# FFN's way down in a decoder layer: half chunk's weights padded to 128 rows, a quarter of the casts on GpSimd

## Chip, cores and metric

One core of a Trainium2 chip runs the whole kernel in one launch. The metric is the device time in microseconds. Engines are called as the profile calls them: PE (TensorE matmul), PEld (TensorE weight load), DVE (VectorE), ACT (ScalarE), POOL (GpSimd), SP (SyncE, which only issues DMAs here).

## What is computed

A decoder layer over x of shape 4 x 1024 x 256: windowed causal self-attention, cross-attention to 77 context rows, and a quantised feed-forward network (FFN) with 704 hidden units. The change touches the FFN's last matrix product alone. The reference, cut to the FFN:

```python
def _act_fake_quant(x, clip_factor):
    scale = sigmoid(clip_factor) * max(abs(x)) / 127
    return clip(round(x / scale), -128, 127) * scale

xq = _act_fake_quant(layernorm(x), clip_x[0])          # 4 x 1024 x 256
gate = xq @ weight_quant(w_gate).T                     # 704 hidden units
up = xq @ weight_quant(w_up).T
h = _act_fake_quant(silu(gate) * up, clip_down[0])     # one scale over all of h
x = x + h @ weight_quant(w_down).T                     # back to 256
```

The scale of h comes from the largest absolute value of all of h, so the way down can begin only when the last h is there.

## The kernel before

Tokens are cut into 32 tiles of 128; eight groups n of four tiles (512 tokens) go through the FFN. The 704 hidden units are five full chunks of 128 (`FULL` = 5) and a half chunk of 64 (`HR` = 64). The half chunks of two groups, an even n and the odd one after it, share one slot of 128 rows: rows 0 to 63 belong to the even group, rows 64 to 127 to the odd one. So a pair m of groups has 11 slots in `hT` (float32): slots 0 to 4 and the shared slot 5 are treated with the even group, slots 6 to 10 with the odd one.

The weights of the way down are `wdT`, bf16, 128 rows x 6 chunks x 256. In its sixth chunk the 64 rows of the half chunk stand twice, in rows 0 to 63 and again in rows 64 to 127, so that each group's matmul finds weights on the rows of its own data. They are made by DVE during attention.

Stages of the FFN, as they follow in time: `act_scale` for the input; `gate_up` for n = 0 to 7, in which POOL widens the inputs from int8 to bf16 (L1199); `act_scale` for h; and the way down. The order on each engine is the order of the program text, each engine has its own queue, and engines wait for each other by semaphores.

The way down runs over ten parts: `(0, 2)`, `(2, 2)`, six parts of four tiles (groups 1 to 6), and two parts of two tiles again. For each part `quantised_h` has ACT write int8 (`h8`, L1323) and DVE cast it to bf16 (`hq`, L1324), one instruction of each for a whole part (the first part has one for each of its two tiles). `down` then does six matmuls for each token tile (L1338), with 128 columns of `hq` as weights and 256 columns of `wdT` streamed; two tiles share a PSUM bank `po`. DVE multiplies the bank by the row of scales (L1343). Of the four tiles of a part the first two are then stored by a DMA that adds to the output in memory, issued by POOL (L1347); for the other two DVE adds x (L1349) and SP issues a plain store (L1350). The last two parts both use the second way. `quantised_h` is called one part ahead of `down`, so DVE's queue holds: cast of part k+1, product, product and sum of part k, cast of part k+2. `h8` and `hq` have two buffers each, one for a pair of groups, and `y` has six.

In `down` the sixth matmul of each tile works on 64 rows: the even group's on rows 0 to 63, the odd group's on rows 64 to 127.

Of the kernel before, what the change touches and what calls it, by code (L numbers as in the profile page):

```python
# [9 lines left out]
BF16 = mybir.dt.bfloat16  # L10
# [7 lines left out]
P = 128  # L18
# [6 lines left out]
def decoder_layer(  # L25
# [32 lines left out]
    nc = tc.nc  # L58
    B, S, D = x.shape
# [9 lines left out]
    HT = NT // NH  # L69
# [3 lines left out]
    HR = FF - (NF - 1) * P  # L73
# [66 lines left out]
    wdT = fw.tile([P, NF, D], BF16, name="wdT")  # L140
# [44 lines left out]
    with ExitStack() as att:  # L185
# [14 lines left out]
        for o in range(NS):  # L200
# [15 lines left out]
            q = wp.tile([P, 1], F32, name=f"qrows{o}")  # L216
# [8 lines left out]
        f = stage.tile([P, P], F32, name="cb_f", tag="stage")  # L225
# [198 lines left out]
        def prep_ffn():  # L424
# [61 lines left out]
            for w, dst, sc in ((w_gate, wgT, gsc), (w_up, wuT, usc)):  # L486
                for f in range(NF):
                    pieces.append(rows_of(w, dst, sc, f))
            return pieces + [down(c) for c in range(NC)]


# [646 lines left out]
    with ExitStack() as ffn:  # L1138
        ffn.enter_context(tc.manual_schedule(engines=None))
        fp = ffn.enter_context(tc.tile_pool(name="fp", bufs=1))  # L1140
# [34 lines left out]
        FULL = NF - 1  # L1175
# [44 lines left out]
        def largest(k, h):  # L1220
            nc.vector.tensor_reduce(
                hmax[:, k : k + 1], h, AX.XY, ALU.max, apply_absolute_value=True
            )

        def gate_up(n, steps):
# [34 lines left out]
            elif n < NB - 1:  # L1260
                largest(n, hT[:, m, FULL:, :])

        def rows_out(t0):
            b, t = divmod(t0, NT)
            return out[b, t * P : (t + 2) * P, :].rearrange("(t p) d -> p t d", p=P)


        for t0 in range(0, B * NT - 4, 4):
            nc.sync.dma_start(out=rows_out(t0), in_=xb[t0 // NT][:, t0 % NT : t0 % NT + 2, :])
# [38 lines left out]
        def quantised_h(t0, nt, step):  # L1308

            n, i0 = divmod(t0, HT)  # L1310
            m, odd = divmod(n, 2)
            if m not in pairs:
                shape = [P, 2 * FULL + 1, HS]
                pairs[m] = (
                    fwk.tile(shape, I8, name="h8"),
                    fwk.tile(shape, BF16, name="hq"),
                )
            q8, q = pairs[m]

            fs = slice(FULL + 1, None) if odd else slice(0, FULL + 1)  # L1320
            for i in range(i0, i0 + nt, step):
                s = slice(i * P, (i + step) * P)
                nc.scalar.activation(q8[:, fs, s], hT[:, m, fs, s], AF.Copy, scale=ih)  # L1323
                nc.vector.tensor_copy(q[:, fs, s], q8[:, fs, s])  # L1324
            return q

        def down(q, t0, nt):
            odd = t0 // HT % 2
            half = slice(odd * HR, (odd + 1) * HR)
            for t2 in range(nt // 2):  # L1330
                po = ps_f.tile([P, 2, D], F32, name="po", tag="b")
                for i in range(2):
                    at = (t0 + 2 * t2 + i) % HT
                    s = slice(at * P, (at + 1) * P)
                    for f in range(NF):
                        r = half if f == FULL else slice(0, P)
                        k = FULL if f == FULL else odd * (FULL + 1) + f
                        nc.tensor.matmul(  # L1338
                            po[:, i, :], q[r, k, s], wdT[r, f, :], start=(f == 0), stop=(f == FULL)
                        )  # L1340
                b, t = divmod(t0 + 2 * t2, NT)
                y = fwk.tile([P, 2, D], F32, name="y", bufs=6)
                nc.vector.tensor_tensor(  # L1343
                    y, po, dsc_row.unsqueeze(1).to_broadcast([P, 2, D]), ALU.mult
                )
                if t % 4 == 0 and t0 < B * NT - 4:
                    nc.gpsimd.dma_start(out=rows_out(t0 + 2 * t2), in_=y, accum_op=ALU.add)  # L1347
                else:
                    nc.vector.tensor_tensor(y, y, xb[b][:, t : t + 2, :], ALU.add)  # L1349
                    nc.sync.dma_start(out=rows_out(t0 + 2 * t2), in_=y)  # L1350
# [5 lines left out]
        for i, (t0, nt) in enumerate(parts):  # L1356
            ahead.append((quantised_h(t0, nt, nt if i else 1), t0, nt))
            if i == 0:
                nc.vector.tensor_scalar(dsc_row, dsc_row, sh, nokey, ALU.mult, ALU.add)
            if len(ahead) == 2:  # L1360
                down(*ahead.pop(0))
        down(*ahead.pop(0))


# [47 lines left out]
```

## Time and profile before

| | |
|---|---|
| median of three runs | 717.52 us (715.24 to 720.91) |
| the profiled execution | 717.03 us, its span 715.3 us |
| mean granted PE clock | 0.971 |
| way down, first ACT instruction to last DVE instruction | 678.28 to 711.85 us of the span |
| ACT L1323, 11 instructions | 20.93 us without a break, from 678.28 |
| DVE L1324 casts | 560 ns (768 elements) to 1849 ns (3072 elements), 11 instructions |
| PE L1338 | 192 matmuls, 160 on 128 rows and 32 on 64 rows |
| POOL L1347 | 7 DMA issues, about 1.2 us each |
| POOL L1199, int8 to bf16 | 7 casts of 1024 elements, about 1.04 us each |

The span runs from the first to the last instruction of the profile; the time of the execution holds 1.7 us more. Times in what follows are microseconds from the start of the span. A row of a timeline has the start, the duration, the engine, the line, the operation, output and inputs, shapes and count, and in brackets how long the engine sat idle before it and what it waited for. "issue" means that it waited for nothing that the profile shows. Rows that follow without a hole are merged, and a merged row carries the shape of its first member.

### The profile page before, as it was taken

The numbers are of one execution on the slowest core, as the hardware profiler recorded it, in microseconds if no ns is written. First come the engines' busy times: TensorE is split into PE (matmuls) and PEld (weight loads), VectorE is DVE, ScalarE is ACT, GpSimd is POOL, SyncE is SP. The second block draws the span as 40 slices with busy tenths as digits, with TensorE's granted clock in tenths as the row PEclk, the third lists the DMA queues.
The fourth block names the chain that finished last, engine by engine and source line by source line (L and its number), as shares of the span: only waits on it lengthen the run. The fifth ranks groups of instructions, "written<-read, shape, count | busy, mean of one in ns | idle before, by whom it ended". The sixth has DMA issues, their size and how long they took to land.

```text
span 715.3 us, 17054 instructions
## 1 busy us (share of the span) xinstructions
PE 651.2 (91%) x6337; PEld 393.0 (55%) x6342; DVE 565.7 (79%) x1997; ACT 366.3 (51%) x671; POOL 241.7 (34%) x390
## 2 busy tenths in 40 slices
PE   7989999999999889999998998999999996678396
PEld 4557566667665656654566666544544525334153
DVE  5588879669787898667879978877866788689897
ACT  2534555634656436544564454346345382698391
POOL 4035533535335457600155577113400021111022
PEclk9999999999999999999999999999999999699788
DMA  8000100000000000000000000000000000000057
GB/s 290 5 2 11 35 3 17 2 19 18 24 11 1 10 10 11 18 3 16 3 10 23 25 24 23 3 3 4 17 17 4 17 17 15 1 0 1 0 89 148
DMA packets 18644, 17.00 MB, mean 24 GB/s; under 512 B 3788, under 2 KB 18049, under 8 KB 18561
## 3 DMA queue, kind: packets, MB, share of 16 engines
q1 hardware_dynamic: 16369, 14.08, 6.3%
q0 software_dynamic: 1904, 1.84, 2.1%
q8 instruction: 50, 0.82, 0.5%
q14 instruction: 33, 0.27, 0.1%
q10 hardware_dynamic: 288, 0.00, 0.0%
HBM read 9.35 MB, written 6.03 MB: 22 GB/s over the span
## 4 chain that ended last, share of the span: by engine, by line
PE 71%; DVE 17%; ACT 6%; issue 4%; DMA 1%; POOL 0%; ACTq 0%; DVEq 0%
PE ps_p L570 12%; PE sc_n L614 8%; PE ps_av L743 7%; PE sc_t L699 7%; PE ps_op L793 7%; PE sc_n L629 4%; PE ps_av L753 4%; PE sc_t L728 4%; PE ps_v L551 3%; PE po L1338 3%; PE sc_t L684 3%; DVE junk L644 3%; PE ps_t L529 2%; PE pg L1236 2%; PE sc_n L595 1%
## 5 line engine op out<-in xcount | busy, mean ns | idle before, releaser
L644 DVE CUSTOM_DVE_ANT_0 junk<-sc_n,cboth 128x256 bf16<-128x256 f32 (+1 forms) x512 | 172.8, 403 | 36.8 <-PE sc_n L614 36.5
L709 ACT ACTIVATE pt<-sc_t 128x512 f32<-128x512 f32 (+1 forms) x256 | 125.4, 576 | 100.0 <-PE sc_t L699 99.1
L713 POOL TENSOR_SCALAR_AFFINE_SELECT pt<-pt 128x256 f32<-128x256 f32 x256 | 102.8, 410 | 135.8 <-ACT pt L709 125.1
L731 ACT ACTIVATE ptx<-sc_t 77x512 f32<-77x512 f32 x128 | 65.5, 592 | 78.7 <-PE sc_t L728 78.7
L152 POOL TENSOR_TENSOR r<-ve,neghalf 128x4 f32<-128x4 f32 x22 | 22.6, 1028 | 211.9 <-DVE ve L150 136.7
L699 PE MATMUL sc_t<-q,k 32*128 32x256 f32 (+1 forms) x1024 | 87.2, 380 | 1.4 <-DVE mx L644 0.6
L614 PE MATMUL sc_n<-k,q 32*128 32x256 f32 (+1 forms) x1024 | 81.4, 394 | 1.1 <-DVE mx L644 1.1
L655 DVE TENSOR_REDUCE mx<-sc_n 128x4 f32<-128x308 f32 x128 | 52.2, 470 | 31.2 <-PE sc_n L629 31.2
L699 PEld LDWEIGHTS sc_t<-q,k 32*128 32x128 f32 x1024 | 66.8, 189 | 11.8 <-ACT q L584 2.3
L514 POOL TENSOR_SCALAR xn<-x,mv,rs 128x256 f32<-128x256 f32 x56 | 69.6, 1250 | 7.9 <-DVE rs L163 7.9
L614 PEld LDWEIGHTS sc_n<-k,q 32*128 32x128 f32 x1024 | 49.9, 187 | 31.6 <-DVE mx L644 13.0
L570 PE MATMUL ps_p<-xnT,w_s 128*128 128x512 f32 x128 | 62.5, 618 | 2.3 <-DVE mx L644 1.1
L743 PE MATMUL ps_av<-pt,vt 128*32 128x256 f32 (+1 forms) x1152 | 58.6, 346 | 6.2 <-DVE mx L644 4.4
L762 DVE STREAM_TRANSPOSE o_sb<-ps_av 128x512 f32<-128x512 f32 x64 | 45.7, 715 | 20.2 <-PE ps_av L743 11.8
L743 PEld LDWEIGHTS ps_av<-pt,vt 128*32 128x32 f32 x1152 | 34.8, 109 | 33.7 <-DVE mx L644 6.2
L644 DVE DVE_READ_ACCUMULATOR2_ANT mx<- 128x1 f32 x512 | 42.6, 83 | 0.1
L629 PEld LDWEIGHTS sc_n<-kx,q 32*128 32x128 f32 x1024 | 31.5, 186 | 14.5 <-issue 14.5
L684 PE MATMUL sc_t<-mb_t,ident_bf 77*77 77x512 bf16 x128 | 35.4, 379 | 4.1 <-ACT q L580 3.6
L570 PEld LDWEIGHTS ps_p<-xnT,w_s 128*128 128x128 f32 x128 | 22.5, 192 | 28.3 <-issue 17.3
L1250 DVE SCALAR_TENSOR_TENSOR hT<-pu,usc,act 128x512 f32<-128x512 f32 x44 | 30.6, 744 | 8.7 <-ACT act L1249 5.8
L629 PE MATMUL sc_n<-kx,q 32*128 32x77 f32 x1024 | 36.2, 277 | 0.0
L753 PE MATMUL ps_av<-ptx,vx 77*32 77x512 f32 x256 | 35.2, 604 | 0.5 <-DVE mx L655 0.5
(184 smaller groups left out, 1046.4 us busy)
## 6 DMA issues: line engine op xcount, KB each, us to landing
x<-in_x_dram SPq DMA_DIRECT2D x8, 512.0 KB
out_dram<-y SPq DMA_DIRECT2D x9, 256.0 KB
q<-mxT SPq DMA_DIRECT2D x128, 4.0 KB
out_dram<-x SPq DMA_DIRECT2D x7, 256.0 KB
out_dram<-y POOLq DMA_DIRECT2D x7, 256.0 KB, 4.5
w_s<-in_L_attn_w_qkv_dram SPq DMA_DIRECT2D x2, 384.0 KB
raw_d<-in_L_ffn_w_down_dram SPq DMA_DIRECT2D x2, 352.0 KB
raw_f<-in_L_ffn_w_gate_dram SPq DMA_DIRECT2D x5, 128.0 KB
```

Source lines behind the costliest of these rows:

```text
L514: eng.tensor_scalar(xn, xb[job.b][:, t, :], job.st[hf].mv[:, i, 0:1], job.st[hf].rs[:, i : i + 1], ALU.subtract, ALU.mult,)
L570: nc.tensor.matmul(ps, w[:, c, g * P : (g + 1) * P], job.xnT[hf][:, c, :], start=(c == 0), stop=(c == NC - 1),)
L614: nc.tensor.matmul(banks[j][:, (i + 1) * 2 * P - n : (i + 1) * 2 * P], q[r, t * P : (t + 1) * P], k[r, k0 * P : k0 * P + n], start=True, s ...
L629: nc.tensor.matmul(banks[j][:, i * SK : (i + 1) * SK], q[r, t * P : (t + 1) * P], k[r, :], start=False, stop=(i == HT - 1),)
L644: nc.vector.tensor_tensor_reduce(out=junk[:, 2 * P - n :], in0=banks[j][:, (i + 1) * 2 * P - n : (i + 1) * 2 * P], in1=cboth[:, 2 * P - n ...
L684: nc.tensor.matmul(banks[j][:SK], ident_bf[:SK, :SK], mb_t[:, s], start=True, stop=False)
L699: nc.tensor.matmul(banks[j][:, w : w + n], k[r, t * P : (t + 1) * P], q[r, t * P : t * P + n], start=True, stop=True,)
L709: nc.scalar.activation(pt.rearrange("p i a q -> p (i a q)")[:, :w], banks[j][:, :w], AF.Exp)
L713: nc.gpsimd.affine_select(out=pt[:, :, 0, :], in_=pt[:, :, 0, :], compare_op=ALU.is_ge, fill=0.0, base=0, pattern=[[0, 2], [1, P]], channe ...
L731: nc.scalar.activation(pt, banks[j][:SK], AF.Exp)
L743: nc.tensor.matmul(ps[j * SL : (j + 1) * SL, (a0 - t0) * P : (a1 - t0) * P], slot_of(job.vs[kb // 2][:, kb % 2], heads[j]), job.pts[g, o, ...
L753: nc.tensor.matmul(ps[j * SL : (j + 1) * SL, :], slot_of(vx[:, job.b], heads[j]), job.pts[g, o, j, hf], start=True, stop=True,)
```

## The change

A new tile `wdP` of 128 rows x 2 x 256 in bf16 is set to zero by POOL, and POOL copies into it the half chunk's weights: into its first half the rows 0 to 63, into its second half the rows 64 to 127. In `down` the sixth matmul of a tile then reads all 128 rows of the shared slot of `hq`, and the zeros drop the rows of the other group. In `quantised_h`, in the six parts of four tiles, DVE casts only the first three tiles; POOL casts the fourth. The parts of two tiles are cast by DVE alone, as before.

```diff
+        wdP = fp.tile([P, 2, D], BF16, name="wdP")
+        nc.gpsimd.memset(wdP, 0.0)
+        for k in range(2):
+            r = slice(k * HR, (k + 1) * HR)
+            nc.gpsimd.tensor_copy(wdP[r, k, :], wdT[r, FULL, :])
+
         def rows_out(t0):
...
                 nc.scalar.activation(q8[:, fs, s], hT[:, m, fs, s], AF.Copy, scale=ih)
-                nc.vector.tensor_copy(q[:, fs, s], q8[:, fs, s])
+
+                mine = slice(i * P, (i + 3) * P) if step == HT else s
+                nc.vector.tensor_copy(q[:, fs, mine], q8[:, fs, mine])
+                if step == HT:
+                    nc.gpsimd.tensor_copy(q[:, fs, 3 * P :], q8[:, fs, 3 * P :])
             return q
 
         def down(q, t0, nt):
             odd = t0 // HT % 2
-            half = slice(odd * HR, (odd + 1) * HR)
...
                     for f in range(NF):
-                        r = half if f == FULL else slice(0, P)
                         k = FULL if f == FULL else odd * (FULL + 1) + f
                         nc.tensor.matmul(
-                            po[:, i, :], q[r, k, s], wdT[r, f, :], start=(f == 0), stop=(f == FULL)
+                            po[:, i, :],
+                            q[:, k, s],
+                            wdP[:, odd, :] if f == FULL else wdT[:, f, :],
+                            start=(f == 0),
+                            stop=(f == FULL),
                         )
```

POOL's new instructions stand in its queue as follows: the three that fill `wdP` behind its last work of attention (the power at L921) and ahead of its casts of the inputs (L1199); the cast of part k+1 behind the store issue of part k-1 and ahead of that of part k. The numbers of lines in the text are those of the kernel before.

## The prediction

> **What bounds the kernel now.** The page shows PE at 91% and DVE at 79% of the span, but the edited code runs only in the last 37 us. I read the busy time by windows there first; its columns are the busy time and number of instructions of each engine, then the granted PE clock, the DMA share and GB/s.
>
> ```profile
> core 0: us, PE busy (x) PEld busy (x) DVE busy (x) ACT busy (x) POOL busy (x), PEclk, DMA share, GB/s
> 606.00:678.28 72.28, 47.89 (x253) 22.61 (x258) 60.43 (x76) 49.55 (x83) 7.29 (x7) 0.85 0.00 1
> 678.28:686.60 8.32, 6.33 (x33) 3.36 (x34) 5.80 (x8) 8.32 (x6) 1.41 (x1) 0.67 0.04 5
> 686.60:704.45 17.85, 17.85 (x126) 10.22 (x124) 17.64 (x21) 12.61 (x6) 5.76 (x5) 1.00 0.82 147
> 704.45:711.85 7.40, 5.30 (x37) 2.97 (x36) 6.56 (x10) 0.00 (x0) 1.47 (x2) 0.94 0.86 178
> 711.85:715.30 3.45, 0.00 (x0) 0.00 (x0) 0.01 (x1) 0.00 (x0) 0.00 (x0) 0.50 0.22 76
> ```
>
> From 686.60 to 704.45 both PE (17.85 of 17.85) and DVE (17.64) are full: two engines share the bound. Before that ACT is full: it writes the int8 h and lets everything else wait. The chain of waits says the same, and at its end it goes back to DVE:
>
> ```profile
> 681.50 2.33 ACT h L1323
> ...
> 683.86 1.50 DVE hq L1324
> ...
> 685.41 20.83 PE po L1338 x144
> ...
> 707.59 0.96 DVE hq L1324
> ...
> 708.60 1.81 PE po L1338 x12
> ```
>
> Of PE's 20.83 us, what is work? The timeline of the weight loads:
>
> ```profile
> 684.80 0.09 PEld L1338 LDWEIGHTS <-hq 64*128 64x128 bf16 x1 [0.21 <-issue]
> 685.40 0.44 PEld L1338 LDWEIGHTS <-hq 128*128 128x128 bf16 x5 [0.51 <-DVE hq L1324]
> 686.05 0.66 PEld L1338 LDWEIGHTS <-hq 64*128 64x128 bf16 x6 [0.21 <-issue]
> 686.92 0.65 PEld L1338 LDWEIGHTS <-hq 64*128 64x128 bf16 x6 [0.21 <-issue]
> ```
>
> Six loads fill 0.65 us without a hole, then 0.21 us pass in which PE waits for nothing shown; a token tile takes 0.866 us. A group is named by its first member: the hole stands ahead of the 64-row load (alone at 684.80), and none stands ahead of the five 128-row loads behind it. 24 tiles make 5 us of holes.
>
> DVE's own timeline gives its pitch (start to start) from one cast to the next:
>
> ```profile
> 697.36 1.58 DVE L1324 CAST hq<-h 128x2560 bf16<-128x2560 int8 x1
> 698.86 1.27 DVE L1343 TENSOR_TENSOR y<-po,dsc_row 128x512 f32<-128x512 f32 x2
> 700.16 0.69 DVE L1349 TENSOR_TENSOR y<-y,x 128x512 f32<-128x512 f32 x1
> 700.77 1.85 DVE L1324 CAST hq<-h 128x3072 bf16<-128x3072 int8 x1
> ```
>
> Casts of whole parts start at 686.60, 690.30, 693.76, 697.36 and 700.77, and the first of the last two half parts at 704.45: pitches 3.70, 3.46, 3.60, 3.41, 3.68. Inside one: cast 1.42 to 1.77, the two products 1.31, the sum 0.61.
>
> **The change, part by part.**
>
> *64-row matmul becomes 128-row.* All six matmuls of a tile then have one shape, and the hole ahead of the odd one goes: 0.21 us per tile, so a part of four tiles takes 4 x 0.65 = 2.6 us on PE instead of 3.46. On PE alone that is 24 x 0.21 = 5.0 us. It can't be had: DVE needs over 3 us per part and becomes the only bound. So this edit pays only where DVE waited for PE: the two products of the first two whole parts took 1.42 and 1.43 instead of 1.31 (0.23 in all); in the tail the products at 705.42 and 706.26 led to the sum at 706.98, 1.56 instead of 1.31 (0.25); and the last two tiles' matmuls, on the chain at 708.60, lose two holes (0.41). Sum 0.89.
>
> *DVE casts three of four tiles.* The cast lasts 1523 ns for 2560 elements and 1787 for 3072, so 0.516 ns per element. A quarter of a part is 640 or 768 elements: 0.33 or 0.40 us. Six whole parts are cast so; the first of the six (at 683.86) and the start of the second (at 686.60) are held by ACT's h, which is no earlier, so what is won before 686.60 is worth nothing: ACT's chain from 678.28 covers it (0.35 us if that cover were gone). The other five, from 686.60 on, save 0.40+0.33+0.40+0.33+0.40 = 1.86.
>
> *POOL casts the fourth tile.* L1199 is the same operation, int8 to bf16, on POOL: 1042 ns for 1024 elements, so 0.65 or 0.78 us. Other POOL rows are dearer: the affine select at L713 takes 410 ns for 256 elements (1.23 us for 768), the scaling at L514 1250 ns for 256 (3.1 or 3.75 us). I take L1199, which is nearest in kind and types, and keep the others for the range. POOL's new work per part is 0.7 us beside the 1.2 us of the store's issue (L1347), in a pitch of 3.2: there is room. PE needs the fourth tile 3 x 0.65 = 1.96 us after it starts the part, and it starts when DVE's cast ends, so POOL may be over a microsecond late. PE's wait on POOL has only the next part's matmuls behind it. POOL's cast waits for ACT, and behind it in POOL's queue stands the issue of the preceding part's store; for that nobody waits but the end, as y has six buffers. ACT rewrites a pair's h two pairs on: at 689 it needs POOL's cast of about 686.5, at 694 that of about 692, so it does not wait.
>
> *The two casts at once.* The trace has no POOL cast beside a DVE cast. It does have POOL's store issue running into DVE's casts: at 690.30 and 693.76 by 0.13 to 0.18 us, at 697.36 and 700.77 by 0.27, and those two lasted 1.58 and 1.85 against 1.49 and 1.75. So 0.27 us of overlap cost 0.09. In the new order y's first product, 0.3 us of latency and 1.2 of issue again reach 0.25 us into the next cast; I charge 0.09 to the two casts that did not have it yet (0.18). POOL's cast stands behind that issue, so DVE's cast starts first, POOL's falls at worst behind it, beside DVE's products, and is over 0.7 us after DVE's cast: before the fourth tile is due. I price it at 0. If POOL came first and DVE had to wait for all of it, DVE would lose about 0.6 us per part: 3.0 us over five parts, the other end.
>
> The Trainium skill ("SBUF — State Buffer", section "Who interferes with whom") speaks against the change: a DVE cast that uses two ports and any GpSimd instruction share a port pair, and the later one stands still until the earlier has ended. By that rule whoever starts first decides, and the sum would be the forecast or the second rival below; the 0.09 us above is all that a row here shows of it.
>
> *wdP.* POOL sets 512 elements (rows of L249 and of the identity: 592 ns for 578, 205 for 128, so 0.54) and copies twice 256 (0.26 each by L1199, 1.25 by L514): 1.1 to 3.0 us. POOL has nothing to do from 604.00, after its power at L921, to 615.23, its first cast; these 11 us hide it. Without them xq would be late by that much. DVE's small instructions from 604 to 609 are on the path and may be disturbed: 0 to 1.25, I take 0, since POOL is most likely through while DVE reduces maxima at 605.1 to 606.5. No gain can come from it: nothing is removed there.
>
> *Sum.* 1.86 + 0.23 - 0.18 up to the cast at 704.45 (now 702.54), then 0.25 + 0.41: 2.57 us. The last sum on DVE ends near 709.3 instead of 711.85; behind it the last store needs the same 3.45. SP's other stores leave earlier, DMA's share rises from 0.82 to about 0.9 and still does not bind. The profiled execution took 717.03 us (span 715.3, 1.7 around it): **714.5**. It lies 0.5 below the median of the three runs, 717.52, which would give 715.0.
>
> **Rivals.**
>
> *POOL wins the race.* If POOL's cast starts ahead of DVE's, part after part, 3.0 us are given back: 717.03 - 2.57 + 3.0 = 717.5, no change. For it: the issue ends only 0.25 us after DVE's cast starts, a thin margin. Against: the order of the queues, and that margin repeated in five rows.
>
> *POOL is slow and becomes the bound: slower.* Place: POOL's queue, cast and store issue in turn. By L514 a cast takes 3.1 or 3.75; with 1.2 of issue and 0.1 between, a part takes 4.7 instead of 3.57. From 685.3 the six casts and five issues end at 711.2; then the last whole part's fourth tile (0.8), product and sum (1.3), the last cast (1.0), matmuls (1.5), product and sum (1.4): 717.2 for 711.85, so 717.03 + 5.4 = 722.4. It decides from a cast of about 1.9 us, where POOL's part exceeds 3.2. Against it: L1199's seven casts, all within 1037 and 1044 ns.
>
> *The hole stays.* If it does not come from the shape, PE keeps 0.866 per tile: only 0.2 to 0.3 is won at the start, where the first whole part begins earlier: 716.8. Against: the hole stands ahead of the 64-row load alone, and the same engine's 128-row stream at L1236 shows none.
>
> **How the numbers follow.** Forecast 0.62 (its own range 713.0 to 716.5), POOL first 0.16, slow POOL 0.11, hole stays 0.06, else 0.05. Low end: 2.57 + 0.18 + 0.35 all won is 713.9, less the 1.8 by which the lowest run lay under the profiled one: 712.0. High end: 717.5 for the second case plus 2 of run scatter, which also takes in half of the slow-POOL case: 719.5. One per cent, about what a measurement of this kernel can tell from no change, is 7.2 us; no case reaches it, and only scatter or something unseen would: faster 0.06, same 0.88, slower 0.06.
>
> **What would show it.** Right: PE loads of one shape with no 0.21 hole but with waits on DVE's hq in every part; DVE casts of 1.2 and 1.4 us, pitch near 3.2, no idle time; the cast of the first half part near 702.5; POOL casts of 0.65 to 0.8. Wrong: DVE casts or sums stretched by 0.5 or more, POOL casts over 1.9, PE waiting for POOL, or a later start of the stage at 678.28.

## The result, and the profile after

The changed kernel takes 719.16 us (median of 22 runs) against 717.38 us of the kernel before (22 runs): ratio 1.003, 95% interval 1.0019 to 1.0042. It is slower by about 2 us, where 2.6 us less were forecast. The time lies within the stated range, at its upper end, but the sign is the opposite one. The profiled execution took 719.40 us, span 717.7. The new line numbers: L1330 ACT's int8 write, L1333 DVE's cast, L1335 POOL's cast, L1347 the matmuls, L1356 the products, L1360 POOL's store issue, L1362 the sums.

The busy time by windows of the changed kernel, the columns as before:

```profile
678.00:686.60 8.60, 5.83 (x36) 4.07 (x37) 5.93 (x10) 8.23 (x6) 2.17 (x2) 0.67 0.08 5
686.60:704.45 17.85, 12.66 (x111) 10.22 (x108) 17.71 (x18) 12.70 (x7) 8.66 (x9) 1.00 0.64 118
704.45:714.00 9.55, 5.83 (x49) 4.46 (x48) 9.15 (x13) 0.00 (x0) 2.56 (x3) 1.00 0.87 162
```

PE has fallen from 17.85 to 12.66 us in the middle window, as it should, and did fewer matmuls in it (111 for 126): it waits. DVE is as full as before. The timeline of the weight loads shows the same from PE's side:

```profile
692.91 2.52 PEld L1347 LDWEIGHTS <-hq 128*128 128x128 bf16 x24 [1.55 <-DVE hq L1333]
697.66 2.51 PEld L1347 LDWEIGHTS <-hq 128*128 128x128 bf16 x24 [2.24 <-DVE hq L1333]
```

Twenty-four loads run through in 2.5 us without a hole; the 0.21 us holes are gone, and in the third to sixth whole part PE stands for 1.5 to 2.2 us ahead of them, until DVE's cast is there. DVE's timeline tells where its time went:

```profile
686.82 1.98 DVE L1333 CAST hq<-h 128x2304 bf16<-128x2304 int8 x1
...
690.02 1.02 DVE L1362 TENSOR_TENSOR y<-y,x 128x512 f32<-128x512 f32 x1
690.96 1.89 DVE L1333 CAST hq<-h 128x1920 bf16<-128x1920 int8 x1
692.78 1.27 DVE L1356 TENSOR_TENSOR y<-po,dsc_row 128x512 f32<-128x512 f32 x2
694.08 2.26 DVE L1362 TENSOR_TENSOR y<-y,x 128x512 f32<-128x512 f32 x1
696.26 1.35 DVE L1333 CAST hq<-h 128x2304 bf16<-128x2304 int8 x1
...
702.89 0.69 DVE L1362 TENSOR_TENSOR y<-y,x 128x512 f32<-128x512 f32 x1
703.50 2.32 DVE L1333 CAST hq<-h 128x2304 bf16<-128x2304 int8 x1
```

and POOL's shows what lies beside it:

```profile
686.73 0.85 POOL L1335 CAST hq<-h 128x768 bf16<-128x768 int8 x1 [0.39 <-ACT h L1330]
689.70 1.21 POOL L1360 DMA_DIRECT2D out_dram<-y  x1 [2.12 <-DVE y L1356]
690.44 1.19 POOL L1335 CAST hq<-h 128x640 bf16<-128x640 int8 x1
693.74 1.20 POOL L1360 DMA_DIRECT2D out_dram<-y  x1 [2.11 <-DVE y L1356]
694.48 1.30 POOL L1335 CAST hq<-h 128x768 bf16<-128x768 int8 x1
...
702.56 1.20 POOL L1360 DMA_DIRECT2D out_dram<-y  x1 [2.11 <-DVE y L1356]
703.29 1.30 POOL L1335 CAST hq<-h 128x768 bf16<-128x768 int8 x1
```

In the four later parts POOL's cast starts 0.73 to 0.74 us after its store issue started, not 1.2 us after. That puts it into DVE's sum and ahead of DVE's next cast. At 703.50 DVE's cast of 2304 elements lasts 2.32 us; at 696.26, with no POOL cast beside it, 1.35. At 694.08 it is the sum that lasts 2.26 instead of 0.69. The products, in between, keep their 1.27 for two. In the second whole part no issue stands right ahead of POOL's cast: it waits for ACT and starts at 686.73, 0.09 us ahead of DVE's, which then takes 1.98.

The way down, from ACT's first instruction to the end of DVE's last sum, went from 33.57 to 36.22 us: +0.13 up to the second whole part's cast, +2.99 in the five pitches (17.85 to 20.84), -0.47 in the tail.

### The profile page after: what moved, and what is told of

Its sections match the earlier page's. It is cut to its first block, busy times and chain, and to the rows that moved or that the text cites. A ratio compares the mean times of both kernels' runs of the same rounds, so it can differ in the third digit from the quotient of the medians.

```text
span 717.7 us, 17068 instructions
## 1 busy us (share of the span) xinstructions
PE 647.0 (90%) x6337; PEld 396.1 (55%) x6342; DVE 568.7 (79%) x1997; ACT 366.3 (51%) x671; POOL 247.8 (35%) x399
## 4 chain that ended last, share of the span: by engine, by line
PE 69%; DVE 19%; ACT 6%; issue 5%; DMA 1%; POOL 0%; ACTq 0%; DVEq 0%
PE ps_p L570 12%; PE sc_n L614 8%; PE sc_t L699 7%; PE ps_av L743 7%; PE ps_op L793 7%; PE sc_n L629 4%; PE ps_av L753 4%; PE sc_t L728 4%; PE ps_v L551 3%; PE sc_t L684 3%; DVE junk L644 3%; PE ps_t L529 2%; DVE hq L1333 2%; PE pg L1236 1%; PE sc_n L595 1%
## 5 line engine op out<-in xcount | busy, mean ns | idle before, releaser
L699 PE MATMUL sc_t<-q,k 32*128 32x256 f32 (+1 forms) x1024 | 88.8, 383 | 1.4 <-DVE mx L644 0.6
L514 POOL TENSOR_SCALAR xn<-x,mv,rs 128x256 f32<-128x256 f32 x56 | 69.8, 1255 | 7.9 <-DVE rs L163 7.9
```

Source lines behind the costliest of these rows:

```text
L514: eng.tensor_scalar(xn, xb[job.b][:, t, :], job.st[hf].mv[:, i, 0:1], job.st[hf].rs[:, i : i + 1], ALU.subtract, ALU.mult,)
L699: nc.tensor.matmul(banks[j][:, w : w + n], k[r, t * P : (t + 1) * P], q[r, t * P : t * P + n], start=True, stop=True,)
```

## The experiments

All times are compared with runs of the kernel before on the same chip. "Five pitches" runs from the second whole part's DVE cast to the first half part's; "way down" from ACT's first write to the end of the last sum; both are read from the timeline of one profile.

| kernel | ratio to before, 95% interval | five pitches, us | way down, us |
|---|---|---|---|
| before | | 17.85 | 33.57 |
| changed | 1.003 [1.0019, 1.0042] | 20.84 | 36.22 |
| padding alone | 0.9989 [0.9976, 1.0002] | 17.80 | 33.06 |
| POOL's cast alone | 1.0053 [1.0036, 1.0069] | 21.44 | 37.60 |
| POOL's cast behind DVE's | 0.9966 [0.9951, 0.998] | 16.35 | 31.74 |
| fourth tile on ACT | 0.9985 [0.9971, 1.0] | 16.62 | 32.63 |
| padding, spare cast on POOL | 1.0048 [1.0028, 1.0068] | 22.95 | 39.36 |
| padding, spare zeros on POOL | 1.0028 [1.0014, 1.0043] | 20.99 | 36.23 |
| two tiles on POOL, behind DVE's | 0.9956 [0.9939, 0.9973] | 15.70 | 31.69 |
| one tile behind, halves | 0.9964 [0.995, 0.9979] | 15.95 | 31.08 |
| two tiles behind, halves | 0.9969 [0.9954, 0.9983] | 15.45 | 31.17 |

**The two edits apart.** First the padding alone, then POOL's cast alone:

```diff
-                mine = slice(i * P, (i + 3) * P) if step == HT else s
-                nc.vector.tensor_copy(q[:, fs, mine], q8[:, fs, mine])
-                if step == HT:
-                    nc.gpsimd.tensor_copy(q[:, fs, 3 * P :], q8[:, fs, 3 * P :])
+                nc.vector.tensor_copy(q[:, fs, s], q8[:, fs, s])
```

> The padding alone: the sixth matmul on 128 rows with wdP, DVE casts all four tiles as before, POOL casts nothing. Theory (the loss is DVE and POOL standing in each other's way, and the padding itself is sound): PE loses its 0.21 us holes, 2.6 us per part; DVE's pitch stays at 3.4 to 3.7 with no cast over 1.85; the last sum on DVE ends about 0.9 us earlier than before (0.23 in the first parts, 0.66 in the tail): ratio 0.9985 to 0.9995 of before. Rival (the 128-row matmul or wdP's filling costs time by itself): ratio of 1.002 or more, with the way down starting later or PE late.

> POOL's cast of the fourth tile alone: the sixth matmul stays on 64 rows, no wdP. Theory: the collision needs nothing of the padding, so DVE's casts or sums are stretched by about 1 us per part again (cast and sum together 2.7 to 3.4 instead of 1.75 to 1.95 undisturbed), DVE's pitch is near 4.1, and the ratio is 1.003 to 1.005. Rival (only PE's faster pace brings the two casts into collision): PE stays the bound with 3.46 per part, and the ratio is within 0.001 of 1.

The padding alone has the ratio 0.9989, with an interval that just reaches 1; its way down is 0.5 us shorter in the profile, of the 0.9 expected. POOL's cast alone, on the old matmuls, is slower by 0.5%, a little more than expected, with sums up to 2.26 and casts up to 1.98 us. So the whole loss is the cast's, and PE's faster pace has no part in it.

**POOL's cast behind DVE's.** Same work, other order: a one-column copy makes POOL wait for DVE's cast.

```diff
                 if step == HT:
+                    mk = fwk.tile([P, 1], BF16, name="mk", bufs=2)
+                    nc.gpsimd.tensor_copy(mk, q[:, fs.start, 0:1])
                     nc.gpsimd.tensor_copy(q[:, fs, 3 * P :], q8[:, fs, 3 * P :])
```

> The changed kernel with one thing added: ahead of each cast of a fourth tile POOL copies one column that DVE's cast of the same part has just written, so POOL's cast can only start when DVE's cast is done and falls beside DVE's products from PSUM. Theory (the order of start decides): DVE's casts last 1.2 to 1.4 us, its sums 0.69, its pitch is 3.1 to 3.3, POOL's casts last 0.65 to 0.9, and the sum of the prediction is got back: 2 to 3 us below before, ratio 0.9955 to 0.998. Rival (POOL's cast costs DVE the same wherever it lies, or POOL's longer queue makes the stores late): the pitch stays near 4 and the ratio is 1.002 or more.

Ratio 0.9966: 2.4 us faster than before by the medians (714.83 and 717.25); the way down is 1.8 us shorter in the profile. DVE's and POOL's timelines of this kernel:

```profile
691.43 1.26 DVE L1358 TENSOR_TENSOR y<-po,dsc_row 128x512 f32<-128x512 f32 x2
692.73 0.69 DVE L1364 TENSOR_TENSOR y<-y,x 128x512 f32<-128x512 f32 x1
693.34 1.47 DVE L1333 CAST hq<-h 128x2304 bf16<-128x2304 int8 x1
```

```profile
691.64 0.18 POOL L1336 COPY mk<-hq 128x1 bf16<-128x1 bf16 x1 [1.32 <-DVE hq L1333]
691.76 0.71 POOL L1337 CAST hq<-h 128x640 bf16<-128x640 int8 x1
692.43 1.19 POOL L1362 DMA_DIRECT2D out_dram<-y  x1
```

POOL's cast now lies beside DVE's products and takes 0.71 us (1.19 at its place in the changed kernel). From the second whole part on every sum takes 0.69 and the casts 1.35 to 1.49, of which some 0.1 stands where a store issue still reaches into the cast; only the first whole part's sum is still stretched, to 1.08, with POOL's first cast beside it. The casts are longer than the 1.2 to 1.4 expected, for a reason that the last experiments show. One instruction of 0.18 us turned a loss into a gain: the place of POOL's cast in time was the cause.

**The fourth tile on ACT.**

```diff
-                    nc.gpsimd.tensor_copy(q[:, fs, 3 * P :], q8[:, fs, 3 * P :])
+                    nc.scalar.copy(q[:, fs, 3 * P :], q8[:, fs, 3 * P :])
```

> The changed kernel with the fourth tile's cast on ACT instead of POOL, right behind ACT's int8 write of the part. Theory (it is POOL that holds DVE up): DVE's casts last 1.2 to 1.4 us and its sums 0.69 again; but ACT gets 0.8 or 0.9 us more per part and becomes the bound with 3.2 to 3.8 per part, ending near 704 instead of 699; the ratio is 0.997 to 1.000. Rival (the loss comes from PE or DVE waiting for a second engine's part of hq, whichever engine it is): casts and sums are stretched here too, ratio 1.002 or more.

Ratio 0.9985. DVE's casts are 1.36 to 1.46 and its sums 0.69. A second engine's share of `hq` does no harm as such; DVE now waits a little for ACT, which has become longer.

**What is held, and by what.** On top of the padding alone, with DVE casting everything, POOL casts the fourth tile into a spare tile, or only sets the spare tile to zero:

```diff
+                if step == HT:
+                    sc = fwk.tile([P, FULL + 1, P], BF16, name="sc", bufs=2)
+                    sc = sc[:, : FULL + 1 - odd, :]
+                    nc.gpsimd.tensor_copy(sc, q8[:, fs, 3 * P :])   # or: nc.gpsimd.memset(sc, 0.0)
```

> The padding, DVE casting all four tiles, and POOL casting the fourth tile once more into a spare tile that nothing reads: POOL's cast at its place in the changed kernel, with none of the relief. Theory (DVE pays about the whole recorded length of POOL's cast, 1.2 to 1.3 us, in a held-up cast or sum): DVE's pitch goes from 3.56 with the padding alone to 4.5 to 4.9, cast and sum together 3.1 to 3.9, ratio 1.006 to 1.010. Rival (PE's or DVE's wait for POOL's part of hq is what costs): nothing waits for this cast, so the pitch stays near 3.56 and the ratio below 1.

> As the run with the spare tile, but POOL sets the spare tile to zero instead of casting into it: an instruction that writes 640 or 768 elements and reads nothing, behind the store issue again from the third whole part on. If any POOL instruction holds DVE up: casts and sums are both stretched as with the cast, by 0.6 to 0.8 us per part, ratio 1.002 to 1.005. If the collision needs POOL's reading for the one and its writing for the other: DVE's sums (which read two tiles) stay at 0.69 while its casts are stretched, pitch about 4.0, ratio 1.000 to 1.004. If a POOL instruction that only writes holds nothing: pitch 3.56, ratio 0.998 to 1.000.

The spare cast, for which nobody waits, costs DVE 22.95 - 17.80 = 5.15 us in five pitches, 1.03 per part. Its ratio of 1.0048 lies below what was expected (the interval reaches to 1.0068), although the pitch (4.59) is as expected and the way down is 6.3 us longer than with the padding alone. In that profile the way down began at 676.2 us, in the ten others between 677.7 and 679.2. Why it began early here is not settled. With zeros in place of the cast, DVE's timeline, and POOL's row that lies beside the first cast of it, read:

```profile
694.59 0.69 DVE L1363 TENSOR_TENSOR y<-y,x 128x512 f32<-128x512 f32 x1
695.20 2.63 DVE L1332 CAST hq<-h 128x3072 bf16<-128x3072 int8 x1
697.75 1.27 DVE L1357 TENSOR_TENSOR y<-po,dsc_row 128x512 f32<-128x512 f32 x2
699.05 0.69 DVE L1363 TENSOR_TENSOR y<-y,x 128x512 f32<-128x512 f32 x1
699.66 2.26 DVE L1332 CAST hq<-h 128x2560 bf16<-128x2560 int8 x1
```

```profile
694.98 1.23 POOL L1336 MEMSET sc<- 128x768 bf16 x1
```

All sums keep 0.69, while the casts of the last four whole parts are held by 0.7 to 0.8 (1.85 and 1.58 with the padding alone). POOL's setting of zeros, which only writes, holds DVE's casts; POOL's cast, which reads too, also holds the sums, which read two SBUF tiles. The products, which read PSUM and one SBUF tile, are not held even where POOL's cast lies right beside them, as in the kernel with the waiting cast. This agrees with the Trainium skill ("SBUF — State Buffer", section "Who interferes with whom"), which has the same three cases.

**How much fits, and five slots.** Two tiles of four on POOL, behind DVE's cast; then, in both kernels that wait, DVE's casts of five slots written as two halves of columns:

```diff
-                mine = slice(i * P, (i + 3) * P) if step == HT else s
+                mine = slice(i * P, (i + 2) * P) if step == HT else s
```

```diff
-                nc.vector.tensor_copy(q[:, fs, mine], q8[:, fs, mine])
+                wide, narrow = q[:, fs, mine], q8[:, fs, mine]
+                if odd:
+                    wide, narrow = (
+                        a.rearrange("p k (i c) -> p i k c", i=2) for a in (wide, narrow)
+                    )
+                nc.vector.tensor_copy(wide, narrow)
```

> The kernel with POOL's cast made to follow DVE's, but with two tiles of four on POOL and two on DVE. DVE's cast falls by another 0.33 to 0.40 us; POOL's takes 1.3 to 1.5 us and no longer fits into the 1.31 us of DVE's two products, so it runs into the sum by 0.2 to 0.5 us. Theory (start order decides, room beside the products is what may be given to POOL): the sum is stretched to 0.9 to 1.2 and eats most of the gain; ratio within 0.001 of that with one tile, 0.9955 to 0.998. Rival (POOL's share is free once it starts behind DVE's cast): pitch 2.9 to 3.0, sums 0.69, ratio 0.993 to 0.995.

> The kernel with POOL's cast behind DVE's and one tile of four on POOL; in addition DVE's casts of five slots (the odd groups) are written as two halves of the columns times five slots instead of five slots, the same elements. In the runs so far five slots of 384 columns took 1.36 us, as long as six slots of 384, and five slots of 256 took 0.96, as long as six of 256. Theory (DVE goes through the outermost dimension in two halves at once, and five leaves one half empty for a fifth of the elements): 1920 elements take 1.36 x 5/6 = 1.13 to 1.18 and 1280 take 0.80 to 0.85; DVE's pitch over five parts falls from 3.27 to about 3.19, the tail by another 0.2, some 0.6 us in all, ratio 0.995 to 0.997. Rival (the time of a cast goes by the length of a run or has a step of its own): 1.36 and 0.96 stay or grow, ratio as without it or worse.

> The same halves in the kernel with two tiles of four on POOL. Theory: DVE's casts of 1280 elements take 0.80 to 0.85 instead of 0.96, but in the whole parts POOL's cast of two tiles (1.25 us for 1280 elements) fills the products' 1.3 us and still holds DVE's sum, so only part of it is won; ratio 0.993 to 0.996. Rival (POOL sets the pitch, its cast, marker and store issue filling it): no gain over two tiles without the halves, ratio 0.9955 or more.

With two tiles on POOL its cast takes, after the first part, 1.25 to 1.47 us and runs past the products; DVE's sums rise to 0.83 to 1.32, and the way down is 31.69 instead of 31.74 us long: nothing more to win there. With the halves on top its ratio is 0.9969, outside the 0.993 to 0.996 expected and where the rival put it, although the way down is 0.5 us shorter in the profile. The ratios of the four kernels in which POOL waits, taken on three chips, can't be told apart (0.9956 to 0.9969). Their casts can. Groups by form, of the kernel with one tile on POOL and then of the same with halves; the columns are busy time and mean duration in ns, then idle time before:

```profile
L1333 DVE CAST hq<-h 128x2304 bf16<-128x2304 int8 x3 | 4.3, 1427 | 0.0
L1333 DVE CAST hq<-h 128x1920 bf16<-128x1920 int8 x3 | 4.3, 1418 | 0.5 <-ACT h L1330 0.5
```

```profile
L1338 DVE CAST hq<-h 128x2304 bf16<-128x2304 int8 x3 | 4.3, 1429 | 0.0
L1338 DVE CAST hq<-h 128x1920 bf16<-128x1920 int8 x3 | 3.6, 1216 | 0.5 <-ACT h L1330 0.5
```

1920 elements in five slots cost as much as 2304 in six; as two halves of five slots they cost 0.2 us less, and the undisturbed one, in the first whole part, 1.16, close to five sixths of 1.36. The Trainium skill ("VectorE: DVE Perf Modes", section "Mode 2×_2P — use both read ports for one tensor") says that such an operation is split in halves along its outermost dimension; the rows fit a split of five slots into three and two, the longer setting the time.

## Why the prediction was wrong

**The step that failed** is "The two casts at once": "POOL's cast stands behind that issue, so DVE's cast starts first" and "I price it at 0". The issue's recorded 1.2 us were taken for the time in which POOL can't start anything else. POOL started its cast 0.74 us after the issue began, which is 0.40 to 0.42 us into DVE's sum and 0.2 us before DVE's next cast would have started. The margin of 0.25 us that the text called thin had the other sign, in four parts; in the second whole part POOL's cast, waiting for ACT with no issue ahead, came first by 0.09 us, a case that the prediction does not look at. The Trainium skill ("GPSIMD Engine Reference", section "2.1 Instruction dispatch") states that a Pool instruction's completion does not hold back the next Pool instruction. The rows agree: POOL's cast starts 0.74 us into an issue recorded with 1.20.

**The rival "POOL wins the race" was the right one, at too low a price.** (It is the first in the list; the passage on the skill calls it the second.) It was given 0.6 us per part and so ended at no change. The five pitches were forecast at 15.94 and took 20.84, 4.90 more. Of these, 4.49 are gone when POOL's cast is put behind DVE's: 0.90 per part. Two things were not in the price: POOL's cast itself is stretched to 1.19 to 1.30, and DVE's sum is held as well as its cast.

**The cast's relief was partly mis-sized.** It was taken as 0.33 us for a part of five slots, from a rate per element. Undisturbed, 1920 elements took 1.36 instead of 1.19, so those parts save 0.13 to 0.16. The rate came from five and six whole slots of 512 columns (1.49 and 1.75), where the time does go by the elements. The kernel before also had casts of cut slots, 1536 elements as six slots of 256 columns and 1280 as five:

```profile
681.54 0.96 DVE L1324 CAST hq<-h 128x1536 bf16<-128x1536 int8 x1 [0.58 <-ACT h L1323]
...
707.59 0.95 DVE L1324 CAST hq<-h 128x1280 bf16<-128x1280 int8 x1
```

Five cut slots took as long as six there already. With POOL's cast put behind DVE's, the five pitches take 16.35, 0.41 more than forecast, and the way down is 33.57 - 31.74 = 1.83 us shorter. With the halves, an edit that the prediction did not have, they take 15.95 and the way down is 33.57 - 31.08 = 2.49 us shorter, close to the 2.57 worked out.

**What held.** The holes came from the 64-row shape: 24 loads in 2.52 us where 2.6 was forecast. That PE's 5 us can't be had because DVE is the bound held too: the padding alone wins 0.05 us in the five pitches, which is 0.23 less the 0.18 charged for the store issues that now reach further into two more casts (1.59 and 1.85 where they were 1.49 and 1.75). The tail won 0.47 of the 0.66: the last twelve matmuls went from 1.81 to 1.50, and the last cast took 1.05 instead of 0.95. The first whole part was covered by ACT as said, except that its sum, held to 0.96 by POOL's first cast, made the next DVE cast 0.13 us late. `wdP` is filled from 606.57 on for 1.4 us, later than assumed, and costs nothing that can be seen: from the reduction of xmax to its inverse DVE took 1.86 us instead of 1.83 in the starts. POOL's slow rates of L514 did not apply; undisturbed its cast took 0.71 or 0.82.

**Sums and readings of the prediction that do not come out.** By its own terms the rival of the slow POOL ends its six casts and five issues at 711.9 without any gap, not at 711.2, and stood near 723; the low end of the range comes to 712.1. The issues' reach into the next cast, called repeated in five rows, was 0.13 and 0.18 us in two of them. One per cent was taken for what a measurement can tell; it told 0.3%. None of this bears on the outcome.

Not settled: where the hold falls. In the changed kernel, with POOL's cast alone and with the spare cast, twelve POOL casts started behind a store issue, all 0.40 to 0.42 us into DVE's sum. The six of 640 elements left the sum at 1.01 or 1.02 and held the next cast too; five of the six of 768 held the sum to 2.26 or 2.27 and left the next cast alone; the last one left the sum at 0.69 and held the cast to 2.32. So a sum of two SBUF tiles is not safe for having started first, and "whoever starts first decides" does not carry over from DVE's casts to its sums; why the number of elements matters is not shown.

## What to carry to other kernels

Work that is moved from DVE to POOL must be placed in time, not only counted: put it beside DVE instructions that read PSUM and at most one SBUF tile, and tie its start to the end of the DVE cast it would collide with; here that was worth 0.6% (1.003 to 0.9966). Where two engines are both full, removing the holes of one wins next to nothing until the other is relieved. A price per element holds only for the same shape: here five whole slots were cheaper than six, five cut slots were not.

## What the runs showed of the hardware that was not expected

POOL's store issue is recorded with 1.20 us, yet POOL's next cast or setting of zeros starts 0.73 to 0.74 us after the issue began. POOL writing zeros holds a DVE cast by 0.7 to 0.8 us but leaves a DVE sum of two tiles at 0.69; POOL casting holds both. A DVE cast of five slots of 384 columns takes 1.36 us, as long as six; of five slots of 256 columns 0.96, as long as six; as two halves of columns the five take 1.16 and 0.83.
